# Scaled rows, centred weights and shorter key and norm chains in a fused two-layer Perceiver block

## The chip, the core and the metric

The kernel runs on one core of a Trainium2 chip. The metric is device time in microseconds (us) from the start to the end of the program on that core. Five engines work side by side: TensorE (PE, matmuls into PSUM), VectorE (DVE), ScalarE (ACT), GpSimd (POOL) and SyncE (SP, which issues the DMAs here). Each runs its own instructions in a fixed order and waits on semaphores for the others. In the profile's rows "PEld" is TensorE's weight load.

## The reference: what is computed

The input `x` is 128 batches of 32 rows of 256 values; `ctx` is 128 batches of 257 context rows of 256 values. Everything is float32 at the interface. Six stages are added to `x` one after the other, each of them fed with the layer norm of `x` (mean removed, divided by the standard deviation, no weights):

```python
x = x + _L0_xattn_ref(ctx, ln(x), wq, wk, wv)      # softmax attention of x over ctx
x = x + _L0_attn_ref(ln(x), W_in, ...)             # gated selective scan, 512 channels x 16 states
x = x + _L0_ffn_ref(ln(x), W_fc, ...)              # MLP 256-1024-256 with ternary weights, GELU, layer norm
x = x + _L1_xattn_ref(ln(x), ctx, ctx, Wq, ...)    # linear attention: focused feature map, 16 heads
x = x + _L1_attn_ref(ln(x), W_q, ...)              # latent attention, 16 heads, decay over distance
x = x + _L1_ffn_ref(ln(x), w1, b1, w2, b2)         # MLP with ternary weights, inputs rounded to 8 bits
```

Three details matter here. The scan keeps for every channel 16 states `h = h*exp(A*d) + x*d*B` over the 32 rows and sums them with a weight for each state. The focused feature map of the linear attention is `p = relu(x) + eps` over a scale, and its result is `p^3 / |p^3| * |p|`; keys and values there come from all 257 context rows, with biases `bk` and `bv`. The last MLP scales each row to its largest absolute value and rounds it to integers of 8 bits.

## The kernel before, in words

**Tiling.** A group is 4 batches, so 128 rows of `x` fill the 128 partitions. There are 32 groups in 9 blocks of 2, 4, 4, 4, 4, 4, 4, 4 and 2 groups (`BLOCKS`). For a block the program writes down first `context_group` for each group (softmax attention over the context, then keys and values of the linear attention), then one `scan_block` for the whole block (up to 512 columns at once), then `latent_group` for each group (`mlp`, `linear`, `attention`, `quantized_mlp`).

**Order.** Nothing runs in the order in which it is written. A `Recorder` collects every operation with its reads and writes, and `order()` (lines 415-563) places them one by one in a plan: each stage of each group has a due span in the table `DUE`, each operation a cost from `ns_of` (lines 43-93), and the engine that can start first takes the ready operation that is due first. Some operations may go to one of two engines (`R.either`, `minus_column`, `copy`, `relu`, `scaled`): `chosen` (line 486) takes the engine for which start time plus cost times one plus `PRICE` is smallest. Prices before are 45.2 for DVE, 8.0 for ACT and 6.9 for POOL, so DVE is taken only if the others are far behind. All instructions are issued from line 587 in `trace()`, so in the profile nearly every row reads L587 and is told apart by its tiles. Where the plan leaves PE idle for over 600 ns, line 574 puts in bfloat16 matmuls that compute nothing of use (rows with `onesb,identb`).

**The functions that the change touches.**

- `cubed` (777): `p^3 / |p^3| * |p|` for rows `u`. ACT squares `u` and sums it (`ks`, `ls` are its outputs), POOL multiplies the square with `u`, ACT squares and sums again, POOL raises both sums to the powers +1/2 and -1/2 in one instruction (`kn<-kn,halves`, 4 elements for keys; `ln<-ln,halves`, 2 elements for queries) and multiplies them (`kf`, `lf`).
- `stats` and `norm` (973, 981): DVE's `bn_stats` and `bn_aggr`, POOL's `rstd` (an add and a power), and in `norm` the tile `xn`, by DVE from two per-row scalars: minus the mean, times `rstd`. `scan_block`, `attention` and `quantized_mlp` use `norm`; `context_group`, `mlp` and `linear` use `stats` with weights from which the mean over the input rows was taken once, at the start (`centred`, 792), or a subtraction of the mean alone.
- `keys_values` (1134): for one batch, ACT's relu of the key product (`ku<-pkey`), POOL's add of eps (`ku<-ku,e`), `cubed`, then the value product, which ACT scales by `f` in two halves (`vf<-pval,kf`). The matmul `pk` sums keys times values. At the end of `context_group` (1112) DVE picks the heads' own blocks out of `pk` into `kvc` in two instructions.
- `scan_block` (1172): norms of the block's groups, gates, and for 4 chunks of 128 channels 16 states each: ACT's exponential `a`, DVE's scan `h`, and the weighted sum. The first `POOLED` = 2 states (6 in the last two blocks) are weighted and summed on POOL (`h<-h,w_st`, `some<-some,h`), the others on DVE into `acc` in PSUM.
- `linear` (1276): the value bias is added per query row: `den` is copied from PSUM, POOL multiplies it with `bv1`, DVE adds the numerator and multiplies with `zf`.
- `quantize` and `quantized_mlp` (1426, 1458): the row's largest value, the factor `qm`, and the rounding of `xn` in two steps (DVE then POOL).

Of the kernel before, what the change touches and what calls it, by code (L numbers as in the profile page):

```python
# [17 lines left out]
P = 128  # L18
# [24 lines left out]
def ns_of(engine, name, kw, out, ins, n):  # L43

    if engine == "vector":
# [4 lines left out]
        if name == "bn_aggr":  # L50
            return 118
        if name == "reciprocal":
            return 65 + 6.6 * n
        if name in ("tensor_scalar", "tensor_copy", "scalar_tensor_tensor"):
            pointers = sum(is_ap(kw.get(k)) for k in ("scalar1", "scalar2", "scalar"))
            both = name == "scalar_tensor_tensor"
            fast = not both and not any(in_psum(a) for a in (out, ins[0]))
            start = (105 if in_psum(ins[0]) else 65) if both else 92
            return start + (0, 60, 175)[pointers] + (0.52 if fast else 1.04) * n
        return max(75 + 1.04 * n, 150)  # L60
    if engine == "scalar":
        pointers = is_ap(kw.get("scale")) + is_ap(kw.get("bias"))
        if n == BB * (LQ - 1):
            return 655
        rate, start = (0.834, 85) if in_psum(ins[0]) else (0.93, 65)
        return start + 75 * pointers + rate * n + (135 if kw.get("accum_out") is not None else 0)
    if engine == "gpsimd":
        if kw.get("op") == ALU.pow:
            return 400 + 150 * n
        if name in ("memset", "tensor_copy"):  # L70
            return 190 + 0.7 * n
        if name == "tensor_scalar":
            pointers = sum(is_ap(kw.get(k)) for k in ("scalar1", "scalar2"))
            return 195 + 75 * pointers + 0.83 * n
        if n == NH * LQ and shown(ins[1]).ap[-1][0] == 0:
            return 1030
        return 200 + (2.07 if n < 1000 else 1.7) * n
    if engine == "tensor":
# [7 lines left out]
        if not wide:  # L86
            return max(n / 2.4 + 3, 60)
# [180 lines left out]
class Recorder:  # L268
# [79 lines left out]
    def cost(self, engine, name, args, kw, all_reads, all_writes, all_bufs):  # L348
        if True:
            out = kw.get("out", args[0] if args else None)  # L350
            rest = list(args[1:] if "out" not in kw else args)
            rest += [v for k, v in kw.items() if k not in ("out", "accum_out")]
            ins = [a for a in rest if is_ap(a)]
            outs = [a for a in (out, kw.get("accum_out")) if is_ap(a)]
            full = dict(kw)
            if name == "tensor_scalar":
                full |= dict(zip(("scalar1", "scalar2"), args[2:4]))
            if name == "scalar_tensor_tensor":
                full |= dict(zip(("scalar",), args[2:3]))
            if name == "activation":  # L360
                full |= dict(zip(("func",), args[2:3]))
            if engine == "gpsimd" and name == "tensor_tensor":
                full |= dict(zip(("op",), args[3:4]))
            n = size_of(out)
            ns = ns_of(engine, name, full, out, ins, n)
            table = TABLES.get(full.get("func")) if name == "activation" else None
            tensors = [
                a for a in ins if (size_of(a) > 1 or name == "tensor_tensor") and not in_psum(a)
            ]
            locks = engine == "gpsimd" and len(ins) > 0  # L370
            if engine == "vector":
                two = name in ("tensor_tensor", "scalar_tensor_tensor", "tensor_tensor_scan")
                fast = name in ("tensor_scalar", "tensor_copy") and not in_psum(out)
                locks = len(tensors) > 1 if two else fast and len(tensors) > 0 and n > 64
# [228 lines left out]
PRICE = {"tensor": 0.0, "vector": 45.207809, "scalar": 8.002797, "gpsimd": 6.895979, "sync": 0.0}  # L603
WINDOW = 13.504066
SOONER = 0.067879
AHEAD = 0.971922
HORIZON = 1.829143
# [3 lines left out]
def perceiver_kernel(ctx: ExitStack, tc: tile.TileContext, t: dict, out: bass.AP):  # L611
# [30 lines left out]
    nc.gpsimd.memset(halves[:, 1, :], 0.5)  # L642
    ones = cst.tile([P, P], F32, name="ones")
# [96 lines left out]
    bv1 = row("bv1", t["bv1"], D)  # L740
# [36 lines left out]
    def cubed(u, n, tag, inverse=False):  # L777
# [8 lines left out]
        powers = halves[:, 0:2, 0:n] if inverse else halves[:, 1:3, 0:n]  # L786
        R.gpsimd.tensor_tensor(nrm, nrm, powers, ALU.pow)
        f = tiny(f"{tag}f", [P, n])
        R.gpsimd.tensor_tensor(f, nrm[:, 0, :], nrm[:, 1, :], ALU.mult)
# [93 lines left out]
    R.vector.tensor_scalar(p_l[:, 0, :], pkl[:, 0:D], 0.0, None, ALU.max)  # L883
    R.vector.tensor_tensor(p_l[:, 0, :], p_l[:, 0, :], e1, ALU.add)
# [7 lines left out]
    centred(wq1, 2)  # L892

    def late_setup():
# [14 lines left out]
        for dc in range(2):  # L909
# [4 lines left out]
            R.vector.tensor_copy(wkd[:, dc], pd[:, 0:LAT])  # L914

# [57 lines left out]
    def stats(xg):  # L973

        st = tiny("st", [P, 6])
        R.vector.bn_stats(st, xg)
        mv = tiny("mv", [P, 2])
        R.vector.bn_aggr(mv, st)
        return mv, rstd_of(mv[:, 1:2], LN_EPS)

    def norm(xg):
        mv, r = stats(xg)
        xn = t1k([P, D], "xn")
        R.vector.tensor_scalar(xn, xg, mv[:, 0:1], r, ALU.subtract, ALU.mult)
        return xn, mv, r
# [19 lines left out]
    def context_group(b0, xg, kvc):  # L1005
# [101 lines left out]
        for b in range(0, GB, PAIR):  # L1107
            zs = keys(cTs[b : b + PAIR])
            for i in range(PAIR):
                keys_values(cTs[b + i], zs[i], pk[:, :, b + i, :], sums)  # L1110
        v = pk.rearrange("p c b (h k) -> p h c b k", h=2)
        R.vector.tensor_scalar(kvc, v[:, 0], odd[:, 0:1], None, ALU.mult)
        R.vector.scalar_tensor_tensor(kvc, v[:, 1], odd[:, 1:2], kvc, ALU.mult, ALU.add)

# [19 lines left out]
    def keys_values(cT, z, pk, sums):  # L1134
        u = t2k([P, 2, D], "ku")
        R.relu(u, z)
        R.gpsimd.tensor_tensor(u, u, e1.unsqueeze(1).to_broadcast([P, 2, D]), ALU.add)
        f = cubed(u, 2, "k")
        R.first = (len(R.ops) - 3,)
# [10 lines left out]
        for j in range(2):  # L1150
            R.scalar.activation(
                vf[:, j, :, 0:16], pv[:, j * D : (j + 1) * D].rearrange("p (h k) -> p h k", k=16),
# [518 lines left out]
```

## Time and profile before

| | us |
|---|---|
| median of 3 runs | 1727.35 (1726.26 to 1727.77) |
| the profiled execution, its own time | 1720.31 |
| its span in the trace | 1718.6 |
| outside the span (1720.31 - 1718.6) | 1.7 |

| engine | busy us | share of the span | instructions |
|---|---|---|---|
| PE | 1636.2 | 95% | 17465 |
| PEld | 1209.2 | 70% | 17495 |
| DVE | 1513.6 | 88% | 2992 |
| ACT | 1406.5 | 82% | 3441 |
| POOL | 1311.0 | 76% | 2063 |

How to read it: one execution was recorded, and all durations come from it; it took 7.0 us less than the median of the runs. A row of the groups view gives line, engine, operation, `output<-inputs` by tile names (numbers left out), shapes and count, then the busy time, the mean of one instruction in ns, and the idle time of that engine just ahead of it with what ended it. A busy PE counts up to the modelled end of each matmul, with its pipeline, so 95% does not mean that its array is 95% full. ACT loads a function table 92 times (1283 ns each), and the SyncE queue needs between 0.3 and 1.1 us for each DMA that it issues.

### The profile page before, as it was taken

The numbers are of one execution on the slowest core, as the hardware profiler recorded it, in microseconds if no ns is written. First come the engines' busy times: TensorE is split into PE (matmuls) and PEld (weight loads), VectorE is DVE, ScalarE is ACT, GpSimd is POOL, SyncE is SP. The second block draws the span as 40 slices with busy tenths as digits, with TensorE's granted clock in tenths as the row PEclk, the third lists the DMA queues.
The fourth block names the chain that finished last, engine by engine and source line by source line (L and its number), as shares of the span: only waits on it lengthen the run. The fifth ranks groups of instructions, "written<-read, shape, count | busy, mean of one in ns | idle before, by whom it ended". The sixth has DMA issues, their size and how long they took to land.

```text
span 1718.6 us, 45554 instructions
## 1 busy us (share of the span) xinstructions
PE 1636.2 (95%) x17465; PEld 1209.2 (70%) x17495; DVE 1513.6 (88%) x2992; ACT 1406.5 (82%) x3441; POOL 1311.0 (76%) x2063
## 2 busy tenths in 40 slices
PE   9999999999999999999999999999999988888897
PEld 6777667767777777777777777766777656666664
DVE  5499599989997799969999998989999899999787
ACT  4588698979887898979988889888987888777676
POOL 6668667867688678887788777867887789688787
PEclk9999999999999999999999999999999999999999
DMA  8221100110110101000210011001100000000000
GB/s 252 79 76 60 30 28 30 35 58 1 35 57 2 35 14 57 8 30 13 70 29 30 4 45 55 10 30 35 42 35 30 2 11 16 4 5 2 5 9 22
DMA packets 44761, 59.72 MB, mean 35 GB/s; under 512 B 8704, under 2 KB 27008, under 8 KB 44544
## 3 DMA queue, kind: packets, MB, share of 16 engines
q1 hardware_dynamic: 44544, 56.81, 10.4%
q8 instruction: 138, 2.26, 0.6%
q14 instruction: 79, 0.65, 0.1%
HBM read 52.32 MB, written 4.19 MB: 33 GB/s over the span
## 4 chain that ended last, share of the span: by engine, by line
PE 41%; DVE 25%; ACT 16%; POOL 13%; issue 5%; DVEq 0%; POOLq 0%; ACTq 0%
DVE h L587 10%; PE pkey L587 7%; DVE acc L587 7%; PE pval L587 6%; PE pproj L587 5%; POOL ku L587 3%; ACT a L587 3%; PE pT L587 3%; PE pmlp L587 2%; ACT L587 2%; POOL some L587 2%; PE pk L587 2%; ACT ks L587 2%; PE pqa L587 2%; POOL rstd L587 1%
## 5 line engine op out<-in xcount | busy, mean ns | idle before, releaser
L587 DVE TENSOR_TENSOR_SCAN h<-a,pproj 128x512 f32<-128x512 f32 (+1 forms) x576 | 615.9, 1087 | 21.6 <-ACT a L587 11.2
L587 ACT ACTIVATE a<-dl,a_neg 128x496 f32<-128x496 f32 (+1 forms) x576 | 368.9, 665 | 82.7 <-DVE h L587 79.3
L587 DVE SCALAR_TENSOR_TENSOR acc<-h,w_st,acc 128x512 f32<-128x512 f32 (+1 forms) x436 | 299.2, 686 | 0.9
L587 PE MATMUL pval<-wkv,cT 128*128 128x256 f32 x1024 | 243.5, 383 | 2.8 <-DVE x L587 1.8
L587 PE MATMUL pkey<-wkv,cT 128*128 128x256 f32 x1024 | 238.1, 386 | 0.0
L587 ACT ACTIVATE ks<-ku 128x256 f32<-128x256 f32 x512 | 209.2, 414 | 13.6 <-POOL ku L587 10.2
L587 PEld LDWEIGHTS pkey<-wkv,cT 128*128 128x128 f32 x1024 | 189.3, 190 | 37.9 <-issue 14.8
L587 PEld LDWEIGHTS pval<-wkv,cT 128*128 128x128 f32 x1024 | 188.3, 190 | 35.3 <-issue 4.5
L587 POOL TENSOR_TENSOR ku<-ku,e 128x512 f32<-128x512 f32 x128 | 164.9, 1298 | 42.9 <-ACT ku L587 41.6
L587 POOL TENSOR_TENSOR ku<-ks,ku 128x512 f32<-128x512 f32 x128 | 163.2, 1283 | 20.5 <-ACT ks L587 18.9
L587 POOL TENSOR_TENSOR kn<-kn,halves 128x4 f32<-128x4 f32 x128 | 131.2, 1027 | 17.9 <-ACT ks L587 16.7
L587 ACT ACTIVATE vf<-pval,kf 128x256 f32<-128x256 f32 x256 | 107.8, 474 | 30.8 <-PE pval L587 17.5
L587 POOL TENSOR_TENSOR rstd<-rstd,halves 128x1 f32<-128x1 f32 x224 | 124.3, 558 | 7.0
L587 PE MATMUL pproj<-xTs,w_in 128*128 128x512 f32 (+1 forms) x288 | 123.7, 554 | 1.3 <-ACT vf L587 0.7
L587 ACT ACT_TABLE_LOAD x91 | 116.8, 1283 | 2.0 <-PE ph L587 0.5
L587 PE MATMUL pmlp<-w_pr,hT 128*128 128x256 f32 x512 | 116.8, 381 | 1.5 <-ACT hT L587 1.2
L587 POOL TENSOR_TENSOR some<-some,h 128x512 f32<-128x512 f32 (+1 forms) x104 | 115.1, 1107 | 3.1
L587 POOL TENSOR_SCALAR h<-h,w_st 128x512 f32<-128x512 f32 (+1 forms) x104 | 65.0, 628 | 60.4 <-DVE h L587 50.1
L587 POOL TENSOR_SCALAR rstd<-mv 128x1 f32<-128x1 f32 x224 | 45.5, 203 | 84.7 <-DVE mv L587 56.1
L587 PEld LDWEIGHTS pmlp<-w_pr,hT 128*128 128x128 f32 x512 | 95.8, 190 | 17.0 <-ACT hT L587 2.1
L587 ACT ACTIVATION_READ_ACCUMULATOR ks<-ku 128x1 f32 x512 | 100.1, 195 | 0.0
L587 ACT ACTIVATE ku<-pkey 128x512 f32<-128x512 f32 x128 | 73.0, 592 | 14.8 <-PE pkey L587 11.7
(289 smaller groups left out, 3836.1 us busy)
## 6 DMA issues: line engine op xcount, KB each, us to landing
cx<-in_ctx_dram SPq DMA_DIRECT2D x64, 512.0 KB
x<-in_x_dram SPq DMA_DIRECT2D x32, 128.0 KB
cr<-in_ctx_dram SPq DMA_DIRECT2D x128, 32.0 KB
out_dram<-x SPq DMA_DIRECT2D x32, 128.0 KB
vlz<-vl SPq DMA_DIRECT2D x128, 1.1 KB
w_in<-in_w_inT_dram SPq DMA_DIRECT2D x1, 1024.0 KB
raw_fc<-in_w_fcT_dram SPq DMA_DIRECT2D x2, 512.0 KB
raw_pr<-in_w_prT_dram SPq DMA_DIRECT2D x2, 512.0 KB
```

Of the source, the lines that this page charges most:

```text
L587: ins = getattr(engine, name)(*(traced(a) for a in args), **{k: traced(v) for k, v in kw.items()}).ins
```

## The change

The edits, by part:

1. **Centred weights, rows only scaled.** `w_in`, `w_gate`, `wqa` and `wkd` are centred once at the start. `scan_block` and `attention` then need no mean: `xn` is the row times `rstd`, on DVE, POOL or ACT, as the plan chooses. In `scan_block` the `rstd` of all groups of the block come from one pair of POOL instructions, after the moments of all groups.
2. **Quantized MLP.** `xn` is the row minus its mean (DVE or POOL); the factor `rstd` is multiplied into `amax` and into `qm`; the two rounding steps may go to either engine.
3. **`cubed`.** One sum is inverted by DVE, multiplied with the other on either engine, and POOL raises half as many elements to the power 1/2.
4. **Keys.** For the first of each group's four batches (`WHOLE`), DVE does relu and the add of eps in one instruction from PSUM, in place of ACT and POOL. The scaling of the values `vf` may also go to DVE as one instruction.
5. **Value bias.** It is added to `kvc` once per group (two instructions of 128 elements, on either engine), not per query row; `kvc`'s first half may go to ACT. The bias arrives in 16 small DMAs in place of one.
6. **Scan.** A third state goes to POOL (not in the last two blocks), and its weighting may run on ACT.
7. **`mlp`.** The two halves of the float32 rows are multiplied in another order.
8. **The planner.** Cost figures, prices (26.0 for DVE, 4.3 for ACT, 3.7 for POOL), window, and the whole `DUE` table are new, so that the order of all instructions differs.

```diff
@@ cubed
-        powers = halves[:, 0:2, 0:n] if inverse else halves[:, 1:3, 0:n]
-        R.gpsimd.tensor_tensor(nrm, nrm, powers, ALU.pow)
         f = tiny(f"{tag}f", [P, n])
-        R.gpsimd.tensor_tensor(f, nrm[:, 0, :], nrm[:, 1, :], ALU.mult)
+        R.vector.reciprocal(f, nrm[:, 1 - inverse, :])
+        R.either.tensor_tensor(f, f, nrm[:, inverse, :], ALU.mult)
+        R.gpsimd.tensor_tensor(f, f, halves[:, 1, 0:n], ALU.pow)
@@ set-up
-    bv1 = row("bv1", t["bv1"], D)
+    bvc = wts.tile([P, 2, 16], F32, name="bvc")
+    for c in range(2):
+        for h in range(8):
+            h_ = slice((c * 8 + h) * 16, (c * 8 + h + 1) * 16)
+            R.sync.dma_start(bvc[h * 16 : (h + 1) * 16, c, :], t["bv1"][:, h_].to_broadcast([16, 16]))
...
+    centred(w_in, 2)
+    centred(w_gate, 2)
+    centred(wqa, 2)
...
+        centred(wkd, 2)
@@ norms
-    def norm(xg):
-        mv, r = stats(xg)
+    def normed(xg, r):
         xn = t1k([P, D], "xn")
-        R.vector.tensor_scalar(xn, xg, mv[:, 0:1], r, ALU.subtract, ALU.mult)
-        return xn, mv, r
+        R.record({
+            "vector": ("tensor_scalar", (xn, xg, r, None, ALU.mult), {}),
+            "gpsimd": ("tensor_scalar", (xn, xg, r, 1.0, ALU.mult, ALU.mult), {}),
+            "scalar": ("activation", (xn, xg, AF.Copy), {"scale": r}),
+        })
+        return xn
@@ context_group, keys_values
-        R.vector.tensor_scalar(kvc, v[:, 0], odd[:, 0:1], None, ALU.mult)
+        R.scaled(kvc, v[:, 0], odd[:, 0:1])
         R.vector.scalar_tensor_tensor(kvc, v[:, 1], odd[:, 1:2], kvc, ALU.mult, ALU.add)
+        vb = t1k([P, 2, GB, 16], "vb")
+        R.either.tensor_tensor(
+            vb, bvc.unsqueeze(2).to_broadcast([P, 2, GB, 16]),
+            kvc[:, :, :, 16:17].to_broadcast([P, 2, GB, 16]), ALU.mult,
+        )
+        R.either.tensor_tensor(kvc[:, :, :, 0:16], kvc[:, :, :, 0:16], vb, ALU.add)
...
-        R.relu(u, z)
-        R.gpsimd.tensor_tensor(u, u, e1.unsqueeze(1).to_broadcast([P, 2, D]), ALU.add)
+        e12 = e1.unsqueeze(1).to_broadcast([P, 2, D])
+        if whole:
+            R.vector.scalar_tensor_tensor(u, z, 0.0, e12, ALU.max, ALU.add)
+        else:
+            R.relu(u, z)
+            R.gpsimd.tensor_tensor(u, u, e12, ALU.add)
@@ scan_block
         for g in range(size):
-            xn, _, _ = norm(x[g])
+            moments(x[g], mvs[:, g])
+        R.gpsimd.tensor_scalar(rs, mvs[:, 0:size, 1], LN_EPS, 1.0, ALU.add, ALU.mult)
+        R.gpsimd.tensor_tensor(rs, rs, halves4[:, 0:size], ALU.pow)
+        for g in range(size):
+            xn = normed(x[g], rs[:, g : g + 1])
...
-                    R.gpsimd.tensor_scalar(h, h, weight, 0.0, ALU.mult, ALU.add)
+                    R.record({
+                        "gpsimd": ("tensor_scalar", (h, h, weight, 0.0, ALU.mult, ALU.add), {}),
+                        "scalar": ("activation", (h, h, AF.Copy), {"scale": weight}),
+                    })
@@ linear, quantized_mlp
-        den = tiny("den", [P, NH], 2)
-        R.vector.tensor_copy(den, pv[:, :, 16])
...
-        R.gpsimd.tensor_tensor(
-            yv, bv1.rearrange("p (h k) -> p h k", k=16),
-            den.unsqueeze(2).to_broadcast([P, NH, 16]), ALU.mult,
+        R.vector.tensor_tensor(
+            yv, pv[:, :, 0:16], zf.unsqueeze(2).to_broadcast([P, NH, 16]), ALU.mult
         )
-        R.vector.tensor_tensor(yv, pv[:, :, 0:16], yv, ALU.add)
-        R.vector.tensor_tensor(yv, yv, zf.unsqueeze(2).to_broadcast([P, NH, 16]), ALU.mult)
...
-        R.vector.tensor_scalar(m, m, 127.0, None, ALU.mult)
+        R.either.tensor_scalar(m, m, 127.0, unit, ALU.mult, ALU.mult)
...
-        engine = wide if n == HID else R.vector
+        engine = wide if n == HID else R.either
...
-        xn, mv, r = norm(xg)
+        mv, r = stats(xg)
+        xn = t1k([P, D], "xn")
+        R.minus_column(xn, xg, mv[:, 0:1])
...
+        R.either.tensor_tensor(amax, amax, r, ALU.mult)
+        q, dq = quantize(xn, D, msq, 1.0, amax, g1, late, r)
@@ constants
-PRICE = {"tensor": 0.0, "vector": 45.207809, "scalar": 8.002797, "gpsimd": 6.895979, "sync": 0.0}
+PRICE = {"tensor": 0.0, "vector": 25.953779, "scalar": 4.343922, "gpsimd": 3.720799, "sync": 0.0}
...
+WHOLE = (0,)
-POOLED = 2
+POOLED = 3
```

## The prediction

> **What bounds the kernel now.** I read the page's busy shares first, then the chain that ended last, then busy time by stage, then the groups of DVE, POOL and ACT by shape, and last the waits.
>
> ```profile
> PE 1636.2 (95%) x17465; PEld 1209.2 (70%) x17495; DVE 1513.6 (88%) x2992; ACT 1406.5 (82%) x3441; POOL 1311.0 (76%) x2063
> ...
> PE 41%; DVE 25%; ACT 16%; POOL 13%; issue 5%; DVEq 0%; POOLq 0%; ACTq 0%
> ```
>
> No engine owns the chain: PE holds 41%, the other three 54%. Busy time by stage (each engine's busy us and count; I cut where the first full block has begun, and where the context work ends):
>
> ```profile
> 0.00:172.00 172.00, 166.22 (x1610) 127.68 (x1614) 122.10 (x276) 113.81 (x356) 117.53 (x187) 1.00 0.37 116
> 172.00:1376.00 1204.00, 1176.23 (x12658) 871.78 (x12671) 1087.95 (x2020) 1036.93 (x2537) 916.30 (x1424) 1.00 0.10 30
> 1376.00:1719.00 343.00, 293.73 (x3205) 209.77 (x3212) 303.54 (x698) 255.80 (x552) 277.13 (x454) 1.00 0.03 9
> ```
>
> The columns are stage, length, PE, PEld, DVE, ACT, POOL. In the middle stage (B, 1204 us) PE is idle for only 1204 - 1176.2 = 27.8 us, DVE is 90% busy, ACT 86%, POOL 76%. In the last (C, 343 us) PE idles 49 us and DVE is fullest. The clock is granted in full (1.00), so it costs nothing. The rows that carry the sums (counts and mean ns ahead of the idle time):
>
> ```profile
> L587 DVE TENSOR_SCALAR xn<-x,mv,rstd 128x256 f32<-128x256 f32 x96 | 46.7, 495 | 7.3 <-POOL rstd L587 5.9 <-POOL msq L587 0.9 <-PE pT L587 0.4
> L587 DVE TENSOR_SCALAR xn<-xn,qm 128x256 f32<-128x256 f32 x32 | 18.3, 572 | 0.2
> L587 DVE SCALAR_TENSOR_TENSOR acc<-h,w_st,acc 128x512 f32<-128x512 f32 x348 | 257.8, 741 | 0.6
> L587 POOL TENSOR_TENSOR kn<-kn,halves 128x4 f32<-128x4 f32 x128 | 131.2, 1027 | 17.9 <-ACT ks L587 16.7
> L587 POOL TENSOR_TENSOR ku<-ku,e 128x512 f32<-128x512 f32 x128 | 164.9, 1298 | 42.9 <-ACT ku L587 41.6 <-PE pT L587 0.5
> L587 ACT ACTIVATE a<-dl,a_neg 128x496 f32<-128x496 f32 x448 | 307.8, 711 | 61.2 <-DVE h L587 59.0 <-DVE qm L587 0.2
> ```
>
> **DVE, removed.** 96 norms `xn`: 46.7. Third state, 24 chunks of 512 at 0.741 and 4 of 256 at 0.470: 19.7. `kvc`'s first half (32 x 0.348): 11.1. `den` copy 5.2, `y` add 13.0, `y` times `zf` now read from PSUM like `oa` (32 x (0.524 - 0.413)): 3.6. `qm` times 127 (64 x 0.142): 9.0. `xn` times `qm`: 18.3. Together 126.6 us. **Added:** the keys of 32 batches from PSUM, at the row of the same kind that reads PSUM (`pproj`, 0.751): 24.0. Reciprocals (128 + 33) x 0.154 (row `qm<-top`): 24.8. Centring in stage A, by `mean<-pmean` (0.416 for 256 columns) and `w_pr` minus mean (2.30 for 2048): 6.9. Net -70.9 us of 1513.6. This takes the free choices as going elsewhere: DVE's price makes a 0.285 us scaling (row `e<-isp`, 128x256) count 7.7 us against 2.3 on POOL, so DVE is taken only if both others start 5 us later. If every free choice fell to DVE, some 100 us would come back and DVE would gain nothing.
>
> **POOL.** Powers of 2 elements, not 4 (0.726 by row `ln`, not 1.027), and 1, not 2 (0.558, not 0.726): -38.5 - 5.5. Add of eps in 32 batches: -41.5. Bias times `den`: -20.4. One `rstd` pair for each block (1.23 for four, not 4 x 0.761; 0.93, not 1.52): -13.9. Added: the third state's sum (24 x 1.275 + 4 x 0.729) 33.5; the quantized MLP's subtraction as in `xc` (0.617) 19.7, its first rounding (0.479, row `h` of 256) 15.3, `qm` (0.24, between the rows of 0.203 and 0.346) 15.4, `amax` (0.199) 6.4; the bias of `kvc`, two adds of 128 elements at about 0.48 (between 0.218 for 2 and 0.744 for 256) 30.7; half of the 64 scalings `xn` at 0.479, 15.3. The 132 weightings of states cost 83.9 us if all on POOL (65.0 now); with half of them there, -23. Sum about -7.
>
> **ACT.** Relu of 32 batches -18.9; `kvc` 32 x 0.36 (between 0.253 and 0.471) +11.5; half of the scalings at 0.414, +13.2; half of the weightings at the rows of `a` (0.711 and 0.502), +43.2. Sum +49, and +6 if POOL keeps the weightings. Plan costs for a weighting are nearly equal on both (3.3 us with price), so I keep both ends. Values `vf` may go to DVE, at its price only when ACT is late; counted at nothing. The 91 table loads of 1.283 us follow from the order; I take them as they are, and ten more or fewer are 13 us of ACT.
>
> At one place a rule speaks against the change. The row says that a state costs DVE 0.741 us, and POOL 0.694 + 1.275 = 1.97 us. The Trainium skill, GPSIMD Engine Reference, Engine selection, wants elementwise work on VectorE, since GpSimd takes about twice as long for two inputs. The ratio agrees here (1275 to 741 is 1.7), and by the rule alone the third state would add 28 x 1.2 us of engine time and be a loss; it counts as one only if POOL became the fullest engine.
>
> **The stages.** About three quarters of the edits lie in B (69 of 96 `xn`, 408 of 576 scans, 400 of 512 squares). *B:* DVE falls by 0.75 x (126.6 - 48.8) = 58 to 1030. ACT rises by 37 to 1074, or by 4 to 1041. If the stage's length follows its fullest engine it becomes 1204 x 1074/1088 = 1188.5 (-15.5) or 1204 x 1041/1088 (-52); but PE shows only 27.8 us of idle time to give. I take **-22**, the middle between 15.5 and 27.8, and keep 0 and -52 as ends, since pipelined ends hide some of PE's waiting. *C:* in its first 171 us DVE is 95% busy, and its terms there (5 `xn` at 0.526, 2 groups of `linear` and `quantize`) are 5.7 us in full. In the last 172 us DVE is 82% busy, and its terms (19 `xn` at 0.446, 10 `xn` times `qm` at 0.838, the linear and `qm` terms, less reciprocals) are 24.9; half of them shorten the end, as the chain there moves from engine to engine: 12.5. So **-18**, from 0 to -30.6. *A:* PE gets 6.6 us of centring matmuls (12 of 512 columns at 0.43, the smaller ones 1.4), partly in place of useless ones. SP gets 15 more DMAs at 0.36 to 0.47, 5.4 to 7 us, ahead of `wqa`, later weights and the next `x` and `cx`; A's DVE is half idle. I take **+3**, from 0 to +8.
>
> *New waits.* In `scan_block` the first three groups' `xn` now wait for the moments of the fourth. Behind a waiting `xn` on ACT or POOL stand exponentials or key products; for its transposes wait `xTs`, and then the gates. The product needs all four anyway, so what is lost is the overlap of three groups' scaling, transposes (0.28 each) and copies (0.38): up to 3 us for each of 7 blocks. DVE has scans of the block before as cover. 0 to +21, I take **+3**. The one removed in exchange is the wait of `xn` for `rstd` (5.9 us in its row), which the cheaper power shortens too. DVE's new reciprocals wait for ACT's sums, with scans behind them, for which ACT's `a` wait in turn; POOL's power waited there 16.7 us in all, so 0 to +17, and as the plan puts them where they are due I take 0. DVE's keys wait for PE as ACT's relu did: a quarter of 11.7 us, hidden likewise. The key chain is 0.3 us shorter on POOL for each batch, but goes over to DVE and back, and the products that it feeds show 1.7 us of PE idle for `vf`: nothing. So does the order in `mlp` (2.4 us of idle in its row).
>
> Sum: -22 - 18 + 3 + 3 = -34. The profiled execution took 1720.3, so 1686.3; the median of the runs lay 7.0 higher, so **1693 us**.
>
> A second rule bears on PE's share. The trace has 70% for weight loads beside 95% for matmuls. The Trainium skill, Perfetto Trace Analysis, Identifying the Most-Contended Engine, calls matmul busy time a poor measure and asks for weight-load busy time, while occupancy is fair for the others. By that DVE is the bound and PE's 27.8 us no limit; B would give 52 and the sum would be 1663.
>
> **Rivals.**
> 1. *DVE alone sets the pace.* For: 88%, the highest after PE; 95% in C's beginning. Against: PE has 97.7% in B. B -52, C -30.6, A and wait +4: 1720.3 - 78.6 + 7.0 = 1649.
> 2. *PE is already full.* For: 27.8 us idle in B. Against: PE has 41% of the chain only, and its waits sit behind the others' work. B 0, C -5.7, A and wait +6: 1727.6, no difference.
> 3. *ACT becomes the bound, slower.* The plan gives ACT all weightings (86.3) and scalings (26.5), with 11.5 - 18.9 a rise of 105 us, 79 of it in B: 1116, above DVE's 1088 of now. A weighting waits on ACT for DVE's scan while exponentials stand behind it; ACT waits for `h` already in 102 places (79.3 us). B 1204 x 1116/1088 = +31, C -5.7, A and wait +6: 1758. It decides from some 51 us more on ACT in B, that is 68 in all, with about two thirds of the weightings and half of the scalings there. Against: the prices are level, so a loaded ACT sends them to POOL.
>
> If the free choices are hardly used (weightings and scalings stay on POOL, `xn` times `qm` on DVE), POOL has +31 and DVE -53; B is held by PE as before and C gives 14, not 18: 1697, inside the forecast.
>
> **Chances.** Forecast (1672 to 1715) 0.64, rival 1 0.14, rival 2 0.12 (half of it within 0.2%, half faster), rival 3 0.10. A measurement of this kernel can tell about 0.2%. Faster 0.84, same 0.06, slower 0.10. The range leaves out rival 3 and the far half of rival 1: 1655 to 1724.
>
> **What would show it.** DVE busy near 1443, ACT 1412 to 1456, POOL 1305 to 1327; no row `y<-bv` or `den`; `kn` gone and a power of 2 elements near 0.73; `xn` rows on ACT and POOL; the time up to the last context product shorter by 10 to 30 us, and the rest after it too. A middle stage that keeps its length with PE idle 28 us in it speaks for rival 2; ACT over 1470 with longer waits of `a` on `h` speaks for rival 3. I am wrong if table loads, waits for the fourth group's moments, or PE's hidden gaps move by more than the 34 us.

## The result and the profile after

The changed kernel took **1731.51 us** in the median of 20 runs (1727.64 to 1736.04), the kernel before on the same chips 1726.89 us (1721.69 to 1727.77, 20 runs): ratio 1.003, 95% interval 1.0022 to 1.0039. It became slightly slower, where 1693 us was forecast. The profiled execution has a span of 1726.0 us, 7.4 more than the one of before.

Part of these 4.6 us goes with the clock that TensorE was granted, a mean over each run that is recorded with it. Runs of one and the same kernel differ by it: 12 runs of the kernel before with a clock of 0.998 or 0.999 took 1720.0 to 1721.3 us, 7 with 0.994 or 0.995 took 1725.7 to 1727.0. The changed kernel's 20 runs took 1727.6 to 1728.9 us at 0.994 and 1734.5 to 1736.0 at 0.986 and 0.987. A straight line through each kernel's runs (53 and 20) falls by 1.4 and by 0.9 us for each 0.001 of the clock, and at 0.994 the two lines are 1.6 us apart. Below, "at like clock" means a run's time less the value of such a line at that run's own clock. It is good to some 2 us (at 0.996 the kernel before took 1722.5 to 1725.9), and it is a reading and not a test, since a kernel can bring about its own clock.

Busy shares and the chain of waits of after, from its page:

```profile
PE 1637.6 (95%) x17429; PEld 1206.8 (70%) x17429; DVE 1460.1 (85%) x2879; ACT 1453.3 (84%) x3576; POOL 1275.6 (74%) x2160
...
PE 32%; ACT 25%; DVE 24%; POOL 13%; issue 5%; DMA 1%; POOLq 0%; DVEq 0%; ACTq 0%
```

The engine sums went the way that the change says: DVE -53 us, POOL -35, ACT +47. (Records of one engine overlap and the page counts the overlap once. Summed by rows, as the forecast's terms are, it is DVE -68, POOL -35, ACT +77.) The time didn't follow. In the chain ACT went from 16% to 25% and TensorE from 41% to 32%. The same three stages of after (stage, length, then busy PE, PEld, DVE, ACT, POOL, the granted clock, DMA share, GB/s):

```profile
0.00:172.00 172.00, 164.68 (x1569) 125.75 (x1570) 125.64 (x288) 112.16 (x357) 102.29 (x183) 1.00 0.37 116
172.00:1376.00 1204.00, 1176.50 (x12644) 866.56 (x12643) 1040.18 (x1946) 1063.58 (x2617) 897.47 (x1497) 1.00 0.10 30
1376.00:1719.00 343.00, 293.93 (x3196) 212.68 (x3194) 293.35 (x644) 275.89 (x604) 274.81 (x482) 0.97 0.03 8
```

In the middle stage DVE fell by 48 us and POOL by 19, ACT rose by 27, and TensorE did about the same work in these 1204 us (12644 matmuls against 12658). A window of fixed length can't show where time went; the last of the 1024 value products of the context can (first and last start in us, of before, then of after):

```profile
L587 PE MATMUL pval<-wkv,cT x1024: 377/379/483, 31.9 to 1465.4; 128*128 128x256 f32 x171
L588 PE MATMUL pval<-wkv,cT x1024: 377/379/792, 30.5 to 1479.5; 128*128 128x256 f32 x171
```

It starts 14.1 us later, and what is left behind it is 6.7 us shorter (253.2 and 246.5 us of the spans). A quarter of these products had started some 6 us later, three quarters under 2 us later, so most was lost in the last quarter of them. (It also shows that the context work doesn't end at 1376 us, where the prediction cut its stages.) In the profile of after the clock was halved for some 13 us between 1387 and 1480 us, in that of before not once until 1699 us: that can be up to 7 of the 14 us.

The groups of after by shape that answer to those of before, then its waits (who waited for whom: us in total, times, longest):

```profile
L588 DVE SCALAR_TENSOR_TENSOR acc<-h,w_st,acc 128x512 f32<-128x512 f32 x324 | 240.5, 742 | 0.5
L588 POOL TENSOR_TENSOR kf<-kf,halves 128x2 f32<-128x2 f32 x128 | 90.5, 710 | 4.4
L588 DVE RECIPROCAL kf<-kn 128x2 f32<-128x2 f32 x128 | 19.5, 154 | 26.3 <-ACT ks L588 24.9 <-POOL kf L588 1.1
L588 POOL TENSOR_TENSOR kf<-kf,kn 128x2 f32<-128x2 f32 x128 | 28.4, 226 | 47.8 <-DVE kf L588 42.6 <-DVE zf L588 3.8 <-DVE mvs L588 0.5
L588 ACT ACTIVATE h<-h,w_st 128x512 f32<-128x512 f32 x57 | 41.0, 721 | 12.0 <-DVE h L588 11.1
L588 ACT ACTIVATE a<-dl,a_neg 128x496 f32<-128x496 f32 x448 | 307.5, 712 | 37.8 <-DVE h L588 35.5 <-DVE mv L588 0.5
```

```profile
ACT a L588 <- DVE h L588: 42.9, 67, 2.3
POOL kf L588 <- DVE kf L588: 42.6, 33, 4.1
POOL some L588 <- ACT h L588: 42.3, 25, 7.3
POOL vb L588 <- DVE kvc L588: 35.9, 16, 11.2
DVE pproj L588 <- ACT some L588: 35.2, 15, 11.6
```

Each instruction costs what its row of before said (0.742 us for a weighted sum, 0.710 for the shorter power, 0.154 for the reciprocal). Where work went over to another engine, new waits stand: POOL for the new reciprocals (42.6 us), POOL for the weightings on ACT (42.3), POOL for DVE in the value bias (35.9). Waits off the path cost nothing, so this list alone doesn't decide; the runs do.

### The profile page after: what moved, and what is told of

It is laid out like the page before. It is cut to its first block, busy times and chain, and to the rows that moved or that the text cites. A ratio compares the mean times of both kernels' runs of the same rounds, so it can differ in the third digit from the quotient of the medians.

```text
span 1726.0 us, 45670 instructions
## 1 busy us (share of the span) xinstructions
PE 1637.6 (95%) x17429; PEld 1206.8 (70%) x17429; DVE 1460.1 (85%) x2879; ACT 1453.3 (84%) x3576; POOL 1275.6 (74%) x2160
## 4 chain that ended last, share of the span: by engine, by line
PE 32%; ACT 25%; DVE 24%; POOL 13%; issue 5%; DMA 1%; POOLq 0%; DVEq 0%; ACTq 0%
DVE h L588 11%; DVE acc L588 5%; PE pproj L588 5%; ACT a L588 5%; PE pkey L588 4%; ACT ks L588 4%; PE pval L588 3%; ACT L588 3%; PE pT L588 2%; PE pmlp L588 2%; POOL ku L588 2%; PE pqa L588 2%; ACT vf L588 2%; POOL rstd L588 2%; PE pka L588 1%
## 5 line engine op out<-in xcount | busy, mean ns | idle before, releaser
L588 DVE SCALAR_TENSOR_TENSOR acc<-h,w_st,acc 128x512 f32<-128x512 f32 (+1 forms) x408 | 280.4, 687 | 0.6
L588 ACT ACTIVATE ks<-ku 128x256 f32<-128x256 f32 x512 | 209.8, 417 | 24.9 <-POOL ku L588 22.0
L588 POOL TENSOR_TENSOR ku<-ks,ku 128x512 f32<-128x512 f32 x128 | 164.1, 1291 | 34.0 <-ACT ks L588 30.3
L588 POOL TENSOR_TENSOR some<-some,h 128x512 f32<-128x512 f32 (+1 forms) x132 | 150.7, 1142 | 46.5 <-ACT h L588 42.3
L588 POOL TENSOR_TENSOR ku<-ku,e 128x512 f32<-128x512 f32 x96 | 123.0, 1291 | 59.9 <-ACT ku L588 55.9
L588 POOL TENSOR_TENSOR rstd<-rstd,halves 128x1 f32<-128x1 f32 x192 | 106.9, 559 | 4.7
L588 POOL TENSOR_TENSOR kf<-kf,halves 128x2 f32<-128x2 f32 x128 | 90.5, 710 | 4.4
L588 DVE BATCH_NORM_STATS2 st<-x 128x6 f32<-128x256 f32 x192 | 78.5, 414 | 9.7 <-POOL x L588 8.5
L588 POOL TENSOR_SCALAR rstd<-mv 128x1 f32<-128x1 f32 x192 | 38.2, 199 | 61.4 <-DVE mv L588 39.1
L588 PE MATMUL ph<-w_fc,xT 128*128 128x512 f32 x256 | 75.4, 423 | 0.8 <-DVE xT L588 0.7
```

The lines of the kernel that those rows point to most:

```text
L588: ins = getattr(engine, name)(*(traced(a) for a in args), **{k: traced(v) for k, v in kw.items()}).ins
```

## The experiments

**Theory.** No engine sets the pace. Four engines work off fixed queues and wait for each other in a circle, so work taken off one of them turns into waiting for the next, and what counts is the order of the queues. **Rivals:** TensorE is full; ACT has become the bound; the changed operations cost more on the chip than their rows.

### One engine at a time

Four kernels keep the order, the engines and the number of instructions of after, and shorten instructions of one engine as they are issued, so that part of the computation is left out. The edit of the first; the others name other operations at the same place:

```diff
+                    R.small = (lambda a: a[:, 0:64] if a.shape[1] > 64 else a) if s in (8, 9, 10) else None
...
+                    R.small = None
@@ trace: after the order is fixed
+                if op.small and (name != "matmul" or not kw["start"]):
+                    args = [
+                        op.small(a) if is_ap(a) and (name != "matmul" or k != 1) else a
+                        for k, a in enumerate(args)
+                    ]
```

> The changed kernel with every instruction in its place and on its engine, but DVE's weighted sum into acc of states 8, 9 and 10 works on 64 columns in place of 512 or 256; part of the sum is left out. By the rows of the changed kernel DVE loses 84 x (0.742 - 0.21) + 24 x (0.474 - 0.21) = 51 us. If PE's queue is full (my rival 2) the time stays at 1.003 of before, within 5 us. If DVE were still the bound, it falls by 35 to 50 us. If the engines hold each other by turns in fixed orders, it falls by 5 to 25.

> The changed kernel with the same order, but ACT's exponentials a of states 8, 9 and 10 cover 2 batches in place of 16 or 8; the rest of a keeps older values. ACT loses 84 x (0.712 - 0.26) + 24 x (0.501 - 0.26) = 44 us. If ACT took DVE's place as the bound (the mechanism of rival 3), the time falls by 30 to 44 us. If PE's queue is full, it stays within 5 us. If the engines hold each other by turns, it falls by 5 to 25.

> The changed kernel with the same order, but POOL's product of square and row (ku from ks and ku) of every second batch covers 64 columns of each half in place of 256. POOL loses 64 x (1.291 - 0.33) = 61 us. If POOL bounds nothing but the end, the time falls by under 8 us; by turns, 5 to 25; if the key chain on POOL were what PE waits for, over 30.

> The changed kernel with the same order, but the second half of the value product (pval) works on 64 columns in place of 256; part of the values is left out. PE loses 512 x about 0.10 = 50 us. If PE's queue is full, the time falls by 35 to 50 us. If another engine sets the pace, it stays within 8 us; by turns, 10 to 30.

Measured, each against the kernel before on the same chips (1726.89 us for the first row, 1722.85 for the others, so ratios are to be compared and not the times). What was cut is less than expected, since the shortened instructions took 0.275, 0.348 and 0.467 us where 0.21, 0.26 and 0.33 had been assumed; their rows:

```profile
L596 DVE SCALAR_TENSOR_TENSOR acc<-h,w_st,acc 128x64 f32<-128x64 f32 x108 | 29.7, 275 | 0.1
L596 ACT ACTIVATE a<-dl,a_neg 128x62 f32<-128x62 f32 x108 | 36.1, 348 | 12.2 <-DVE h L596 11.3 <-DVE mv L596 0.5
L596 POOL TENSOR_TENSOR ku<-ks,ku 128x128 f32<-128x128 f32 x64 | 29.9, 467 | 13.0 <-ACT ks L596 12.5
```

| cut | taken off, us | time, us | ratio to before (95%) | to after at like clock, us |
|---|---|---|---|---|
| none | | 1731.51 | 1.0030 (1.0022 to 1.0039) | |
| DVE | 44 | 1725.68 | 1.0013 (1.0003 to 1.0023) | -6.3 |
| ACT | 32 | 1729.73 | 1.0035 (1.0021 to 1.0049) | -3.0 |
| POOL | 52 | 1729.04 | 1.0035 (1.0022 to 1.0048) | -3.2 |
| TensorE | 43 | 1729.34 | 1.0041 (1.0026 to 1.0056) | -5.3 |

By the ratios only the cut of DVE gave anything, 3 us of 44. But the kernel before had a clock of 0.996 there, in the median, and the cuts 0.990, the one of TensorE 0.987. Against runs of after at like clock each cut gave some 3 to 6 us, a seventh of what it took off or less. Neither reading has an engine that sets the pace. The theory had wanted 5 to 25 us from each (10 to 30 for TensorE), so it was off too: singly, an engine's time is mostly worth less than that.

The cut of TensorE, its page's busy shares and chain:

```profile
PE 1594.9 (92%) x17400; PEld 1183.8 (69%) x17429; DVE 1461.2 (85%) x2879; ACT 1451.8 (84%) x3576; POOL 1272.7 (74%) x2160
...
DVE 31%; PE 25%; ACT 23%; POOL 15%; issue 6%; DMA 1%; DVEq 0%; SPq 0%; POOLq 0%; ACTq 0%
```

TensorE worked 43 us less and the time hardly moved; its share of the chain went from 32% to 25%, and DVE's from 24% to 31%. So at this order TensorE isn't the bound (rival 2 of the prediction had nearly the right time, 1727.6, for a reason that isn't there), nor is ACT, POOL or DVE.

### All four, and DVE in the kernel before

> All four cuts of the runs before (PE's values, DVE's sums, ACT's exponentials, POOL's products) in one kernel, order unchanged; the same parts of the computation are left out. Singly they gave 0 to 5 us. If the four orders hold each other so that a shorter engine only waits for the next, the four together give 25 to 50 us (0.972 to 0.99 of before). If something outside the four engines sets the time (the DMAs, or a fixed latency between them), they give under 10 us again (over 0.997).

> The kernel before, in its order, with DVE's weighted sums of states 8, 9 and 10 on 64 columns; part of the sum is left out. DVE loses 51 us, as much as the change takes from it. My prediction let DVE's load shorten the time: then this gives 15 to 45 us (0.974 to 0.991). If DVE was not the bound before the change either, under 6 us (over 0.9965).

All four cuts together: 1707.44 us, ratio 0.9915 (0.9899 to 0.9932), 0.0115 or 20 us under after (25 to 50 expected), where the four single ones add up to nothing (0.0017 - 0.0005 - 0.0005 - 0.0011). At like clock it is 29 us against a sum of 18. Busy shares and chain:

```profile
PE 1592.6 (93%) x17400; PEld 1185.8 (69%) x17429; DVE 1418.9 (83%) x2879; ACT 1421.0 (83%) x3576; POOL 1224.0 (72%) x2160
...
DVE 29%; PE 29%; ACT 20%; POOL 14%; issue 6%; DMA 1%; SPq 0%; POOLq 0%; DVEq 0%; ACTq 0%
```

By both readings the four together give more than the sum of the single ones, so the engines hold each other up, and more than the 10 us at most that were expected if something outside them, such as the DMAs, set the time. But even together 171 us of work are worth only 20 to 29 us, a tenth to a sixth. The cut of DVE in the kernel before gave 1719.01 us, ratio 0.9972 (0.9961 to 0.9982): 5 us (7 at like clock) for 44. So the low worth of DVE's time isn't new; the kernel before already had it, behind its 88%.

### The order alone, and the weightings

```diff
-WINDOW = 12.63056
+WINDOW = 10.63056
```

> The changed kernel with the same operations, but the planner's constant WINDOW at 10.63 in place of 12.63, so that ready operations are taken in another order. If the order is what the time hangs on, and the table of due times fits only its own constants, the time rises by 50 to 120 us (1.03 to 1.07 of before) though every engine has the same work. If the amount of work sets it, it stays within 10 us of the changed kernel (1.003).

```diff
+            if set(op.ways) == {"gpsimd", "scalar"} and op.ways["gpsimd"][0][0][0] == "tensor_scalar":
+                op.engine = "gpsimd"
```

> The changed kernel in its order, but all 132 weightings of states stay on POOL; 89 go there from ACT. ACT loses 57 x 0.721 + 32 x 0.505 = 57 us, POOL gains about 55. If ACT has become the bound, the time falls by 15 to 40 us. If the orders hold each other, it stays within 8 us or rises, since POOL's queue is longer (0.999 to 1.012 of before).

The other window of the planner (same operations, nearly the same choice of engines, other order): 1872.77 us, ratio 1.0872 (1.0855 to 1.0888), above the 1.03 to 1.07 expected.

```profile
PE 1705.3 (91%) x17573; PEld 1234.4 (66%) x17604; DVE 1463.3 (78%) x2882; ACT 1480.7 (79%) x3597; POOL 1267.6 (68%) x2152
```

DVE and POOL have the same work as in after (1463 and 1268 us), and it takes 145 us longer by the ratio (some 126 at like clock, where its 0.975 lies outside the line), over twenty times what any cut of one engine moved. It is not a free order of equal rank, though: the planner's own end for it is 1800.8 us, 110 later than for after, it has 16 more table loads (20 us of ACT), and the chip added another 70 us to the plan. So the order matters this much, and the planner knew most of it. All 132 weightings on POOL, at the order of after: 1750.61 us, ratio 1.0161 (1.0144 to 1.0178), more than the 1.012 expected as the most. ACT is 41 us lighter there and POOL 49 heavier, and the time rose by 23 us over after by the ratio (15 at like clock), which doesn't fit ACT as the bound (rival 3 of the prediction).

### Both kernels with an order fitted in the same way

If the order decides, the change can only be judged with orders fitted alike. For both kernels I replaced the planner's order by a list, found by moving single instructions along their queues (or to another engine that the code allows) and replaying the whole program with a cost for each operation:

```diff
-        for i in self.order():
+        for i in self.written():
```

First with the costs that the planner of after has, results a little later:

> The changed kernel with the same operations and the same engines allowed, but its order replaced by one written out, found by moving single instructions along their queues (or to the other allowed engine) and replaying the kernel's own planner costs with the results of DVE 37 ns, of ACT 38 ns and of POOL 20 ns later than the planner takes them (the trace of after has 777 ns from a decay exponential's start to the scan's where the plan has 745) and TensorE 0.6% dearer, as the mean of three cost sets two of which carry random errors of 3 to 4% in every duration. In this replay the changed kernel goes from 1714.5 to 1681, the kernel before from 1734.7 to 1701. Theory (no engine bounds, the order of four in-order queues does, and the order of after was fitted to results that come too early): most of the 33 us arrives, 1695 to 1710, ratio 0.982 to 0.990, and below before_fit by 10 us or more, since with both orders fitted in one way the work taken off counts again. Rival A (the operations of after themselves cost more on the chip than their rows, 27 us in all): after_fit gains too, but stays level with before_fit or above it. Rival B (the order is as good as it can be, and TensorE's 1638 us with its gaps are the bound): 1720 to 1735, no difference.

> The kernel before with the same operations, its order found in the same way from the same cost sets, by as long a search: in the replay 1734.7 to 1701. Theory: it gains too, but less than the replay says since its first order was already fitted to costs that the chip keeps: 1700 to 1720, and above after_fit by 10 us or more. Rival A (the operations of after cost more than their rows): at or below after_fit. Rival B (the order can't give more): 1720 to 1730, no difference.

Measured: after_fit 1700.12 us, ratio 0.9861 (0.9843 to 0.9879); before_fit 1700.81 us, ratio 0.9864 (0.9845 to 0.9883). Both are some 24 us under the kernel before, and the change is worth nothing (+4 us at like clock). That spoke for rival A, against my theory, which had wanted 10 us between them. (The 777 ns of that expectation are those of after alone. Over the four traces a scan that waited for its exponential started some 760 ns after it in the mean and 743 in the median; the plan of after has 745, that of before 783. So this figure was hardly off.) What the replay had said differs: it had 1701 us for before_fit, and the chip's span is 1698.4, but 1681 for after_fit, where the span is 1697.7. The same costs held for the one kernel and were 17 us short for the other.

So I measured the costs in these four traces: for each kind of operation the mean time to the next start on its engine where nothing else held that back, and the mean time to the start of a waiting consumer. Some are far from the planner's figures: ACT's 386 plain copies of 256 columns out of PSUM take 0.37 us, where the plan of after has 0.26 (44 us in all) and that of before 0.30. Summed over all operations of a plan (queue time in us, without table loads; which starts count as held back moves a measured sum by some 3 us for ACT, 16 for DVE and 28 for POOL):

| | plan of before | measured | plan of after | measured |
|---|---|---|---|---|
| DVE | 1491 | 1458 | 1420 | 1402 |
| ACT | 1288 | 1229 | 1248 | 1291 |
| POOL | 1331 | 1361 | 1280 | 1277 |

The new cost figures let ACT's queue seem 40 us shorter than before; on the chip it is 62 us longer. The plan of before charged ACT 59 us too much, that of after 43 too little.

> The changed kernel with the same operations, its order found anew with costs measured in the traces of before, after and the two first fits: for each kind of operation the mean time from its start to that of the next one on its engine where nothing else held that back, and the mean time from its start to that of a waiting consumer on each engine; three cost sets again, two with random additions. In this replay the order of after gives 1759, that of after_fit 1724, the new one 1660 (the kernel before: its own order 1773, before_fit 1748, before_fit2 1687). Theory (the order of the interlocked queues sets the time; the order of after was fitted to costs that the chip does not keep): a further step down, 1640 to 1680. Rival A (the change itself is worth nothing once both orders are fitted alike, as after_fit at 1700.1 and before_fit at 1700.8 had it): level with before_fit2 within 5 us. Rival C (their equality was the chance of two searches): below before_fit2 by 15 us or more, as the replay has it with 27. Rival B (TensorE full, no order helps): 1695 or more.

> The kernel before with the same operations, its order found anew in the same way from the same measured costs by as long a search: in the replay 1773 with its own order, 1748 with that of before_fit, 1687 with the new one. Theory: 1650 to 1690. Rival A (change worth nothing at orders fitted alike): within 5 us of after_fit2. Rival C: above after_fit2 by 15 us or more. Rival B (no order helps further): 1695 or more.

> As after_fit2 (the changed kernel's operations, the same measured costs), from another starting order and with other random moves; its replay ends at 1660.4 (after_fit2 1660.1). If the replay orders orders rightly: 1655 to 1668, and 17 us or more below before_fit3. If after_fit2 was luck: 1675 or more.

> As before_fit2, from the kernel's own order and with other random moves; its replay ends at 1692.4 (before_fit2 1686.7). If the replay orders orders rightly: 1682 to 1698. If the difference of after_fit2 and before_fit2 was luck: 1675 or less.

| order and choice of engines | kernel before, us (ratio) | changed kernel, us (ratio) | difference | at like clock |
|---|---|---|---|---|
| the kernel's own plan | 1726.89 | 1731.51 (1.0030) | +4.6 | +2 |
| fitted to the planner's costs | 1700.81 (0.9864) | 1700.12 (0.9861) | -0.7 | +4 |
| fitted to measured costs | 1685.40 (0.9777; 0.9757 to 0.9798) | 1661.63 (0.9640; 0.9621 to 0.9660) | -23.8 | -21 |
| the same, other start and moves | 1688.98 (0.9793; 0.9779 to 0.9807) | 1662.12 (0.9636; 0.9622 to 0.9651) | -26.9 | -24 |

The two fits to measured costs agree within 0.5 us for the changed kernel and 3.6 for the one before, so the 24 to 27 us between the kernels (21 to 24 at like clock) are no luck of one search. The replays with measured costs ended at 1660.1 and 1660.4 us for the changed kernel and 1686.7 and 1692.4 for the one before, all within 2 to 5 us of the chip's spans (1658.2, 1658.5, 1683.1, 1687.2). Rival A falls: the change is worth 21 to 27 us, and the plan that it came with lost them and a few more. That plan is an order and a choice of engines, and the fit changed both; which of the two lost how much was not tried apart. after_fit2 beats the kernel before by 3.6%. Its busy shares and chain, and its middle stage, then the same of before_fit2:

```profile
PE 1605.9 (97%) x17354; PEld 1204.0 (73%) x17385; DVE 1503.5 (91%) x3056; ACT 1410.2 (85%) x3454; POOL 1260.7 (76%) x2075
...
PE 70%; DVE 13%; ACT 8%; POOL 6%; issue 2%; DMA 1%; SPq 0%; DVEq 0%; POOLq 0%; ACTq 0%
```

```profile
172.00:1376.00 1204.00, 1194.84 (x12939) 892.84 (x12961) 1121.43 (x2135) 1072.27 (x2603) 927.58 (x1506) 1.00 0.10 31
1376.00:1658.00 282.00, 248.68 (x2863) 184.54 (x2869) 255.89 (x619) 230.26 (x511) 230.14 (x390) 0.96 0.02 7
```

```profile
PE 1619.5 (96%) x17382; PEld 1209.2 (72%) x17415; DVE 1520.1 (90%) x3017; ACT 1394.0 (83%) x3421; POOL 1308.0 (78%) x2056
...
PE 67%; DVE 16%; ACT 9%; POOL 5%; issue 3%; SPq 0%; DMA 0%; DVEq 0%; ACTq 0%; POOLq 0%
```

```profile
172.00:1376.00 1204.00, 1191.74 (x12847) 890.60 (x12871) 1125.60 (x2096) 1058.67 (x2584) 945.28 (x1459) 1.00 0.10 31
1376.00:1683.00 307.00, 266.39 (x2916) 193.82 (x2923) 272.08 (x638) 224.25 (x489) 246.26 (x411) 0.96 0.03 9
```

With the fitted orders the chain is TensorE's (70%, 32% in after), the middle stage leaves TensorE only 9.2 and 12.3 us idle, and all other engines do more in the same time: the middle 1204 us hold 1121 us of DVE's work instead of 1040. The fitted order also gives work back to DVE. In the plan of after it takes 1 of the 449 operations that may go to DVE or POOL, and none of the 288 that may go to DVE or ACT; in after_fit2 122 and 50. DVE then does 1503.5 us, only 17 less than in before_fit2; POOL does 47 us less and ACT 16 more.

### Does one engine bound at the fitted order?

The cuts of TensorE and DVE again, at the order of after_fit2:

> The order of after_fit2 with the cut of after_cut_pe: the second half of every context value product works on 64 columns instead of 256 (left out: the other columns), 50 us of TensorE. The chain of after_fit2 lies on TensorE for 70%, and TensorE idles 52 of its 1658 us. If TensorE bounds there: 0.4 to 0.7 of the 50 us arrive, 1627 to 1642. Rival (the four queues interlock at this order too, and no engine bounds): within 6 us of 1661.6, as the same cut at the order of after took 2 us.

> The order of after_fit2 with the cut of after_cut_dve: the sums of states 8, 9 and 10 work on 64 columns (left out: the others), 51 us of DVE, which is busy 91% and holds 13% of the chain. If TensorE bounds: 1656 to 1662, 0 to 0.1 of it. Rival (DVE bounds, as its busy share beside 97% for a pipelined TensorE could mean): 1635 or less.

TensorE: 1645.30 us, ratio 0.9537 (0.9524 to 0.9550). DVE: 1658.01 us, ratio 0.9613 (0.9594 to 0.9632), which can't be told from the 0.9640 of after_fit2 (0.9621 to 0.9660). The cut of TensorE:

```profile
PE 1565.1 (95%) x17385; PEld 1169.5 (71%) x17385; DVE 1501.8 (91%) x3056; ACT 1407.4 (86%) x3454; POOL 1265.2 (77%) x2075
```

and the chain of the cut of DVE:

```profile
PE 74%; ACT 10%; DVE 8%; POOL 5%; issue 2%; DMA 1%; SPq 1%; ACTq 0%; DVEq 0%; POOLq 0%
```

The cut of TensorE, worth 0 to 5 us at the order of after, now takes 16 us off, 0.4 of the 41 that its page shows (0.4 to 0.7 of 50 was expected, and 1645.3 is 3 us above that range); the one of DVE 2 to 4 of 44. TensorE is the tightest engine there, without being alone.

## Why the prediction was wrong

**The step that failed** is in "The stages": "If the stage's length follows its fullest engine", with -22 us for the middle stage and, in the last stage, DVE's terms in full or by half (-18). The work did go: by rows DVE -68 us (-71 forecast), POOL -35 (-7). ACT's term was too small: its rows grew by 77 us (+6 to +49), since 89 of the 132 weightings and 48 of the 64 scalings went to it, where half of each was the upper end. But the stage had no fullest engine that it followed. 44 us off DVE were worth 5 to 7 us before the change and 3 to 6 after it, and as much off another engine no more. By a tenth to a sixth, the 42 us net that the pages show off DVE, ACT and POOL (53.5 + 35.4 - 46.8) come to 4 to 7; the two terms, 40 us in the forecast, should have been about that. In place of 16 us less up to the last context product (-22 and the two +3) the profiles show 14.1 more, and behind it 6.7 less in place of 18.

**What the sum left out** is the order. I treated it as a thing that the edits are laid into. It was written anew with the change, and by the runs it is worth more than all edits: 145 us up by one constant, and, with the choice of engines fitted too, some 40 down in the kernel before and 70 in the changed one. The plans' own ends, which `order()` works out, are 1714.0 us for before and 1690.9 for after. The chip's spans are 1718.6 and 1726.0: 4.6 and 35.1 above them. The plan saw a gain of 23 us (and my sum one of 34), and the chip didn't keep the plan's times. That its cost figures did it is likely and not shown: ACT's queue was 43 us longer than charged, the copies out of PSUM alone make 44, and replays with measured costs met the chip within 5 us. Which of the figures it was I did not try. Nor is it settled why the first fit brought both kernels to the same time, beyond that its costs were 17 us short for the changed one.

**What held, and by luck.** At orders fitted alike the change gave -24 and -27, near the -34 of the sum, but its parts were wrong, so the nearness is luck. The last value product in the second pair of fits, before_fit3, then after_fit3:

```profile
L602 PE MATMUL pval<-wkv,cT x1024: 377/379/634, 37.6 to 1435.8; 128*128 128x256 f32 x171
L603 PE MATMUL pval<-wkv,cT x1024: 377/379/483, 39.8 to 1437.8; 128*128 128x256 f32 x171
```

It starts 2.0 us later with the change (9.6 in the first pair, 1428.9 against 1438.5, where the clock was 0.86 in the last 62.5 us ahead of it), and what follows it takes 220.7 us in place of 251.4 (219.7 in place of 254.2). So the gain lies wholly behind the context, some 31 us and more where 18 were forecast, and the middle stage gave none of its 22. In the first stage a quarter of all value products had started 6 us later in after than in before: a stand-in that is inside the 0 to +8, of which I took 3.

**The waits.** The one for DVE's reciprocals, taken as 0 of up to 17, shows 24.9 us on DVE and 42.6 on POOL; what it costs on the path wasn't tried alone. Two of the signs named at the end are out: table loads fell from 92 to 90, and no wait for the fourth group's moments is over 5 us in all (`POOL rstd <- DVE mvs`, 4.8).

**The rivals.** "PE is already full" named the time and not the cause at the order of after: 27.8 us of idle time were no limit on the kernel, since after_fit2 brings the middle stage's idle down to 9.2 us and shortens the kernel by 68 us of span. At the fitted orders it is nearly right for the middle stage, which the change doesn't shorten there. "DVE alone sets the pace" falls with all cuts of DVE. "ACT becomes the bound": its condition came true (some 68 us more on ACT, two thirds of the weightings), its price not; 32 us off ACT gave 0 to 3, and moving the weightings to POOL made the kernel slower. The rule that I set beside them (the Trainium skill, Perfetto Trace Analysis, Identifying the Most-Contended Engine: go for the engine that is occupied most, and judge TensorE by its weight loads) names DVE at each of these orders. At the planner's orders its cut gave 3 to 7 us of 44. At the one order that TensorE bounds (DVE busy 91%, weight loads 73%) DVE's cut gave 2 to 4 and TensorE's 16, so there the measurement is against the rule.

## What to carry to other kernels

Before pricing an edit in a kernel whose engines are all 75 to 95% busy with a chain split between them, ask for the worth of a microsecond on each engine: a cut of one engine at a fixed order gives it. Here it was a sixth of what was cut or less at the planner's orders, and 0.4 for TensorE at the fitted one. Compare such small differences at like clock. Where a planner writes the order, edits and order have to be judged apart, and the order fitted to durations and result times from the trace; here the same edits were worth +5, -1 and some -25 us with three plans. In this case the chain that lay on one engine (70%) went with a good order and told what to shorten next, and the one that was split (32, 25, 24, 13%) went with an order that could still give 70 us.

## What the runs showed of the hardware

- An engine's busy time isn't its queue's time. An exponential of 496 columns on ACT is busy for 712 ns, yet the next instruction starts 610 ns after it where nothing holds it back (mean of four traces), and a scan that waits for it starts some 760 ns after it. So ACT's sum of busy times overstates what its queue is filled with, and a plan needs the two other figures.
- TensorE's busy time is no measure of its work. It is 1637.6 us in after, 1705.3 with the other window and 1605.9 in after_fit2, but 35, 91 and 23 us of that are the useless matmuls that the kernel puts into the plan's gaps (118, 293 and 74 of them, 56 us and 204 in the kernel before). Without them 1610, 1630 and 1587 us are left for nearly the same matmuls, the second at a mean clock of 0.975 and the others at 0.994. So "27.8 us of idle time" in a stage were no bound on what the whole kernel can give.
- The granted clock moves this kernel's time between runs, as the result's section shows: 0.999 to 0.994 goes with 6 us. In the profile of after it falls to half for stretches of 3 to 7 us, and the mean in its last stage is 0.97 against 1.00 in that of before. It can account for about half of the +4.6 us and not for the 38 us between forecast and result; before_fit2 and after_fit2 are shorter with 0.96 in their last stage.
